# An earlier return of half of the lent adjacency, two loads moved behind other transfers and copies, and four more adjacency passes per node tile in the hyperedge stage

## The chip, the core and the metric

One Trainium2 chip, one core. The metric is device time in microseconds: the median of the runs of one kernel. One execution of each kernel was also taken with the hardware profiler, and all traces here are of such executions. The granted clock of TensorE is given as a share of full speed.

A core has five engines that run their own instruction streams in order: PE (TensorE, matmuls and transposes), DVE (VectorE), ACT (ScalarE), POOL (GpSimd) and SP (SyncE, which here only issues DMAs). ScalarE and GpSimd issue DMAs too. In the profile, SPq, ACTq and POOLq are the issuing instructions on those engines.

## The reference

Four graph layers follow one another on `x` (8 x 2048 nodes x 64 features), with one 2048 x 2048 adjacency matrix `adj` of zeros and ones. After each layer: `x = layernorm(x + layer(x))`.

```python
# layer 0: hypergraph attention (64 hyperedges, H is 2048 x 64), h = x @ W
alpha = softmax over the members of a hyperedge of leaky_relu(h @ a_node)
agg   = einsum('ben,bnf->bef', alpha, h)
beta  = sigmoid(h @ a_gn + agg @ a_ge)                     # per node and hyperedge
all_he = elu(beta * h + (1 - beta) * agg)
coefs1 = softmax over the hyperedges of a node of tanh(elu(agg) @ fcW + fcb) @ av
g     = einsum('bne,benf->bnf', coefs1, all_he)
industry = (adj / deg) @ (x @ W_ind)                       # an adjacency product
out   = softmax-weighted sum of the pair (industry, g)
# layer 1
out   = (dinv * (adj + I) * dinv) @ x @ W.T                # an adjacency product
# layer 2: supports I, adj, 2 adj^2 - I, softmax(relu(EE'))  (E: 2048 x 16)
weights = einsum('nd,dkio->nkio', E, weights_pool)         # a 256 x 64 matrix for each node
out   = einsum('bnki,nkio->bno', x_g, weights) + E @ bias_pool
# layer 3: three steps on v, whose row 0 is first set to a given value
v = relu(concat(v, adj @ v) @ W1.T + b1) @ W2.T + b2
```

## The kernel before

**Data.** The 8 x 64 columns of `x` are handled as four **pairs** `p` of two batches (128 columns), the 2048 nodes as four **chunks** `c` of 512, and a chunk as four tiles `t` of 128 nodes. `adj` stays on the chip, in float32r, as sixteen tiles of 128 x 2048: seven of their own (`LEND = 7`, lines 257 to 262) and eight (`LENT = 8`) in two large tiles `adj_more` with the tags `more0` and `more1`, allocated by `lent_tiles` (L260 to L266), and one more. In an adjacency product the left operand is split in a high and a low float32r part (`split`, L163 to L170: a copy on ScalarE, then a subtraction, the line of which is L168). A product of one pair is 2 chunks at a time, 16 tiles, 2 parts: 64 matmuls of 128 x 512 for half of it, 128 in all.

**What sets the order.** Nearly all instructions of TensorE, and those wrapped in `pin`, stay in the order in which the program writes them (`tc.keep_in_program_order`); a scheduler places the rest, among it most DMAs on SyncE. Two generators share TensorE with the rest of the work. `filler` yields single matmuls of adjacency products in the background; `fill(n)` (L421) takes n of them. Each one also calls `tick` (L318 on), which counts down deferred work: `after(n, f, ...)` runs f after n more matmuls, `later(n, f)` likewise but one after the other. Deferred work is placed by a count of matmuls, not by time, and a filler that has nothing ready yields "wait", in which case a tick passes and no matmul is issued.

**Hyperedge stage (60 to 226 us, L767 to L830).** For each node tile k of 16, and each slot s of it (a slot: the s-th hyperedge of each node), three matmuls make `pz`, then VectorE multiplies it by R (L818), ScalarE takes the exponential, VectorE finishes elu (L820) and weights it, GpSimd adds to `acc`. `fill(3)` (L807), once per tile, and `fill(5)` (L809), once per slot, put background matmuls between. Five slots before the end of a tile `slots(tiles[k + 2], ...)` (L814) prepares the tile after the next: a transpose `pslot` on TensorE, two copies on ScalarE (L288), then the one-hot matrices. `acc` is scattered to memory at the end of a tile.

**Mixing stage (226 to 476 us, L894 to L1104).** For each of 16 (pair, chunk) steps i the industry part is turned and scaled (`mix_ind`), g is loaded and turned (`mix_g`), both get scores (`mix_scores`, `mix_weigh`), and `mix_end` (L957 to L984) turns the mixture back: four transposes `pt`, then an addition on VectorE, the layernorm in steps (`normalized`), then a store of x1 by SyncE (L971). Between these, `fill(8)` or, past step 4, `fill(9)`, four times per step.

The background work in this stage is first the rest of the industry products of layer 0, then layer 1 (L1035): for each pair, two halves of 64 matmuls, tile by tile, from `part[p, c]`. That part is made by `l1_parts` (L986): a load of x1 (L992), a scale on GpSimd 16 matmuls later (L995), a cast in two pieces on ScalarE and VectorE 6 further on (L168). `while (p, t // JT) not in part: yield "wait"` (L1041) holds the generator until the cast of that chunk has been issued. At the end of a half two copies `ut` on ScalarE (L1058) empty the accumulators, and `l1_end` (L1009) follows by `later`: four matmuls `po`, an addition, a layernorm, a store of x2 by SyncE, and `load_xn` (L1028). Its three whole-pair loads of x2 (1 MB each, for the start of layer 2) are issued by ScalarE 14 matmuls later (L1033), once there is `room` for them (set behind the second step of a short loop, `make_el`, which fills 32 + 4 x 16 matmuls).

**Layer 2 (508 to 1263 us)** ends with a loop over 32 slots of per-node weights ("the chunk stage"): for each slot `form` builds weights in `w_half`, which lies in the space of `more0` and `more1` (`lend`, L1511; the adjacency tiles there have been stored to `adj_hbm`), and `multiply` uses them one slot later; `w_half` 0 belongs to even slots, 1 to odd ones. Per chunk, `pick` gathers the sums on VectorE, and `chunk_end` (L1577) stores them (`y_hbm`, L1584), loads them back transposed (L1596) with the residual `xb` (L1590), adds (L1602), squares (L1605), takes the power (L1609 to L1611), scales on VectorE in the last chunk (L1618 for x, L1621 for y) and stores x3 (L1623). `at(slot, period, f)` hangs such pieces on the quarters (periods) of a slot. `load_first` (L1634) loads tiles of x3's pair 0 back for layer 3; `first_turn` (L1630) turns one of its chunks.

What follows the loop (L1678 to L1689) is: the adjacency tiles are allocated again, eight DMAs on GpSimd return the first half of them, then the last chunk's `store` and `load` on SyncE, then eight DMAs on SyncE return the second half.

**Layer 3 (1263 to 1729 us).** `opening` (L1795 on) starts the first adjacency product with the tiles that were never lent; 28 matmuls in, the rest of the last `chunk_end` and `last_constants` are issued, the latter with two constants `more` on SyncE (L116), centred on VectorE (L128 to L132). The part of the product with tiles 7 to 11 uses the first returned half and one tile of the second; `first_turn(3)` (L1832) needs the last chunk of x3.

## Time and profile before

| | |
|---|---|
| median of 3 runs | 1728.79 us (1728.06 to 1730.58) |
| profiled execution, its own time | 1730.81 us |
| its span in the trace | 1729.0 us |
| mean granted clock | 0.989 |

The table of stages, from one view of the trace (busy time of an engine in a stretch, in us; the clock; the mean share in which the 16 DMA engines were busy):

| stretch, us | PE | DVE | ACT | POOL | clock | DMA |
|---|---|---|---|---|---|---|
| 0 to 60, degrees and scores of layer 0 | 40.93 | 43.80 | 13.17 | 22.26 | 0.94 | 0.82 |
| 60 to 226, hyperedges | 146.67 | 144.25 | 84.32 | 133.18 | 0.96 | 0.48 |
| 226 to 251.3, between | 23.56 | 7.66 | 9.99 | 8.50 | 1.00 | 0.48 |
| 251.3 to 476, mixing and layer 1 | 221.06 | 161.31 | 86.01 | 131.01 | 1.00 | 0.42 |
| 476 to 508, end of layer 1 | 26.81 | 14.66 | 7.23 | 8.28 | 0.89 | 0.45 |
| 508 to 1235, layer 2 | 723.30 | 291.59 | 285.63 | 203.82 | 1.00 | 0.39 |
| 1235 to 1282, its end, and layer 3's start | 39.36 | 15.30 | 6.08 | 14.02 | 0.96 | 0.77 |
| 1282 to 1729, layer 3 | 433.71 | 164.47 | 96.68 | 48.88 | 0.99 | 0.17 |

How to read what follows. In the list of waits a line such as "PE pz L172 <- DVE y L820: 5.5, 9, 1.2" says that TensorE, before instructions of line 172 that write `pz`, stood 5.5 us in all, in 9 places, at most 1.2 us in one, and that the last thing to come was VectorE's instruction of line 820. Line 172 is the helper for all matmuls and 175 the one for transposes, so the tile's name tells which they are; numbers are left out of tile names. A timeline line is: start, length, engine, line, operation, out<-in, then how often, and in brackets the idle time ahead of it with what ended it. A line of the view by stretches gives the stretch, its length, busy time (and count) of PE, PEld, DVE, ACT and POOL, the granted clock, the DMA share and GB/s.

### The profile page before, as it was taken

What the parts mean: (1) busy time and instruction counts of PE and PEld (TensorE: products, weight loads), DVE (VectorE), ACT (ScalarE), POOL (GpSimd) and SP (SyncE); (2) the same over time, 40 slices, a digit from 0 to 9 for tenths busy, and PEclk for the clock granted to TensorE, in tenths of its full rate; (3) what the DMA queues carried; (4) which work ended last, traced back from release to release, by engine and by line L of the source; (5) the groups of instructions that cost most, each with busy time, mean ns of one, the idle gap of its engine ahead of it and who ended that gap; (6) DMA issues with size and microseconds to landing.
All of it is one profiled execution on the core that took longest, in us unless ns stands there. A gap on an engine that the chain in (4) does not pass through costs nothing. (4 is left out here: it accounts for less than half of the span.)

```text
span 1729.0 us, 28043 instructions
## 1 busy us (share of the span) xinstructions
PE 1655.4 (96%) x11230; PEld 1208.0 (70%) x11230; DVE 843.0 (49%) x1536; ACT 589.1 (34%) x1033; POOL 569.9 (33%) x516
## 2 busy tenths in 40 slices
PE   6888899999989999999999999999989999999996
PEld 4666666666664444478888778888767877878775
DVE  7789945768742221210136157777533433433332
ACT  1355533344321212111213267878511221212221
POOL 3678845556534543422123001313210200202001
PEclk9899999999999999999999999999999999999998
DMA  9833334444330000027344457675571111211111
GB/s 341 277 134 125 121 131 138 146 147 146 117 118 1 31 31 1 24 71 296 113 134 140 118 137 158 138 168 126 171 242 48 50 55 43 62 48 42 57 43 39
DMA packets 171212, 195.83 MB, mean 113 GB/s; under 512 B 71568, under 2 KB 116368, under 8 KB 169792
## 3 DMA queue, kind: packets, MB, share of 16 engines
q1 hardware_dynamic: 160384, 154.61, 30.3%
q0 software_dynamic: 8544, 30.68, 5.3%
q10 hardware_dynamic: 2144, 8.65, 1.3%
q8 instruction: 90, 1.47, 0.4%
q14 instruction: 50, 0.41, 0.1%
HBM read 126.72 MB, written 67.17 MB: 112 GB/s over the span
## 5 line engine op out<-in xcount | busy, mean ns | idle before, releaser
L172 PE MATMUL ua<-pt,xn 128*128 128x512 f32 x512 | 230.2, 592 | 1.4 <-DVE pt L1177 1.4
L172 PEld LDWEIGHTS ua<-pt,xn 128*128 128x128 f32 x512 | 97.0, 190 | 111.0 <-issue 104.1
L1542 DVE COPY w_half<-pw 128x512 f32<-128x512 f32 x160 | 109.8, 705 | 87.8 <-PE pw L172 87.1
L1538 ACT COPY w_half<-pw 128x1024 f32<-128x1024 f32 x128 | 129.8, 1014 | 58.6 <-PE pw L172 58.5
L172 PE MATMUL py<-w_half,xg 128*32 128x128 f32 x4096 | 142.1, 279 | 3.1 <-issue 3.1
L172 PE MATMUL u<-adj,v0h 128*128 128x512 f32 (+1 forms) x388 | 135.7, 427 | 0.6 <-ACT h L1856 0.6
L172 PE MATMUL u<-adj,v0l 128*128 128x512 f32 (+1 forms) x388 | 125.8, 402 | 0.0
L172 PE MATMUL u<-adj_more,v2h 128*128 128x512 f32 (+1 forms) x388 | 125.7, 402 | 0.0
L172 PEld LDWEIGHTS py<-w_half,xg 128*32 128x32 f32 x4096 | 111.3, 138 | 20.5 <-issue 3.7
L172 PE MATMUL u<-adj_more,v2l 128*128 128x512 f32 (+1 forms) x388 | 124.0, 396 | 0.0
L1183 POOL TENSOR_TENSOR acc<-acc,pt 128x512 f32<-128x512 f32 x60 | 76.4, 1274 | 104.3 <-DVE pt L1177 103.7
L172 PE MATMUL pw<-est,wst 64*128 64x256 f32 x1024 | 109.8, 317 | 0.5 <-ACT w_half L1538 0.4
L1177 DVE TENSOR_SCALAR pt<-pt 128x512 f32<-128x512 f32 x64 | 29.8, 465 | 152.8 <-ACT pt L1176 152.7
L172 PEld LDWEIGHTS pw<-est,wst 64*128 64x128 f32 x1024 | 82.2, 185 | 25.4 <-ACT w_half L1538 18.7
L1757 ACT CAST ar<-fcav 128x512 fp32r<-128x512 f32 x64 | 39.6, 618 | 165.7 <-DMA fcav<-in_adj_t 164.8
L172 PE MATMUL u<-adj_more,v3l 128*128 128x512 f32 (+1 forms) x291 | 93.5, 396 | 2.1 <-DVE v3l L168 2.0
L1758 DVE SCALAR_TENSOR_TENSOR ar<-fcav,ar 128x512 f32<-128x512 f32 x64 | 45.6, 713 | 100.6 <-ACT ar L1757 100.6
L1176 ACT ACTIVATE pt<-s 128x512 f32<-128x512 f32 x64 | 38.0, 598 | 164.8 <-PE s L172 164.8
L172 PE MATMUL u<-adj,v1h 128*128 128x512 f32 (+1 forms) x291 | 94.0, 401 | 0.0
L172 PE MATMUL u<-adj_more,v3h 128*128 128x512 f32 (+1 forms) x291 | 93.1, 398 | 0.0
L172 PE MATMUL u<-adj,v1l 128*128 128x512 f32 (+1 forms) x291 | 92.6, 395 | 0.0
L1727 POOL TENSOR_TENSOR x<-x,rows 128x512 f32<-128x512 f32 x16 | 22.5, 1431 | 211.8 <-PE pt L175 200.5
(409 smaller groups left out, 3288.4 us busy)
## 6 DMA issues: line engine op xcount, KB each, us to landing
fcav<-in_adj_t SPq DMA_DIRECT2D x64, 256.0 KB, 2.9
u_hbm<-ut SPq DMA_DIRECT2D x48, 256.0 KB, 2.8
xg<-u_hbm SPq DMA_DIRECT2D x24, 512.0 KB, 7.0
adj<-in_adj_t POOLq DMA_DIRECT2D x16, 512.0 KB, 7.9
adj_more<-in_adj_t POOLq DMA_DIRECT2D x16, 512.0 KB, 7.9
adj_hbm<-adj_more SPq DMA_DIRECT2D x16, 512.0 KB, 6.1
x_hbm<-r SPq DMA_DIRECT2D x28, 256.0 KB, 2.3
hs_hbm<-st ACTq DMA_DIRECT2D x8, 584.0 KB, 5.9
```

Of the source, the lines that this page charges most:

```text
L172: tc.keep_in_program_order(nc.tensor.matmul(*args, **kw))
L1176: nc.scalar.activation(pt, s, AF.Exp)
L1177: nc.vector.tensor_scalar(pt, pt, 1.0, None, op0=ALU.max)
L1183: nc.gpsimd.tensor_tensor(accs[c], accs[c], pt, ALU.add)
L1538: pin(nc.scalar.copy(dst, pw.rearrange("p j o n -> p n (j o)")))
L1542: pin(copy(dst[:, :, 2 * j:2 * j + 2], bank.rearrange("p o n -> p n o")))
L1727: nc.gpsimd.tensor_tensor(xs, xs, b2.to_broadcast([P, JT, P]), ALU.add)
L1757: nc.scalar.copy(ar, seen_a)
L1758: nc.vector.scalar_tensor_tensor(ar.bitcast(F32), seen_a, 1.0, ar.bitcast(F32), op0=ALU.mult, op1=ALU.not_equal, accum_out=left[:, t, k:k ...
```

## The change

Three edits.

1. `lent_tiles` takes a number, so that each of the two large tiles can be allocated by itself. The first one is allocated, and its eight returning DMAs are issued, in the hook of the last slot (`SLOTS`, period 0), where the even-slot buffer `w_half` 0 has no further use but the product of the slot before; they now are on SyncE instead of GpSimd. The second stays where it was. `load_first(NT - 4, NT - 2)`, a load of two tiles of x3, moves from a hook of the last slot to behind the last chunk's `store` and `load`.
2. The three loads of x2 are no longer issued 14 matmuls after the last store of a pair, but collected, and issued behind the two copies `ut` of a half of layer 1; once the last half is through, at once.
3. In the hyperedge stage four more background matmuls follow each `slots(...)` in the loop.

```diff
-    def lent_tiles():
-
-        tiles = []
-        for i in range(2):
-            more = adj_pool.tile([P, LENT // 2, N], F32R, tag=f"more{i}", name="adj_more")
-            tiles += [column_halves(more[:, k, :]) for k in range(LENT // 2)]
-        return tiles
-
-    adj = [adj_tile(adj_pool, t) for t in range(LEND)] + lent_tiles()
+    def lent_tiles(i):
+
+        more = adj_pool.tile([P, LENT // 2, N], F32R, tag=f"more{i}", name="adj_more")
+        return [column_halves(more[:, k, :]) for k in range(LENT // 2)]
+
+    adj = [adj_tile(adj_pool, t) for t in range(LEND)] + lent_tiles(0) + lent_tiles(1)
...
                 if s == max(0, S - 5) and k + 2 < NT:
                     slots(tiles[k + 2], pps, "mm", 3)
+                    fill(4)
...
+    xn_loads, at_once = [], []
+
+    def begin_loads():
+        while xn_loads:
+            p = xn_loads.pop(0)
+            nc.scalar.dma_start(xn[p], x2_hbm[p][:])
+
     def load_xn():
 
         for p in range(NP - 1):
             if room and done[p] == NCH:
                 done[p] = 0
-                after(14, lambda p=p: nc.scalar.dma_start(xn[p], x2_hbm[p][:]))
+                xn_loads.append(p)
+        if at_once:
+            begin_loads()
...
                 pin(nc.scalar.copy(ut, u[c]))
                 later(6 + 8 * k, lambda p=p, c=c, ut=ut, x1=l1_load(p, c): l1_end(p, c, ut, x1))
+            if (p, g) == (NP - 1, 1):
+                at_once.append(True)
+            begin_loads()
...
-    at(SLOTS, 2, lambda: load_first(NT - 4, NT - 2))
...
+    def return_adj(tiles, eng):
+        for t in tiles:
+            for g in range(2):
+                pin(eng.dma_start(adj[t][g].bitcast(F32), adj_hbm[t - LEND, :, cols(g, N // 2)]))
+
+    def return_first():
+        adj[LEND:LEND + LENT // 2] = lent_tiles(0)
+        return_adj(range(LEND, LEND + LENT // 2), nc.sync)
+
+    at(SLOTS, 0, return_first)
...
     store, load, *waiting = ends[-1]
-    adj[LEND:LEND + LENT] = lent_tiles()
-
-    def return_adj(tiles, eng):
-        for t in tiles:
-            for g in range(2):
-                pin(eng.dma_start(adj[t][g].bitcast(F32), adj_hbm[t - LEND, :, cols(g, N // 2)]))
-
-    return_adj(range(LEND, LEND + LENT // 2), nc.gpsimd)
+    adj[LEND + LENT // 2:LEND + LENT] = lent_tiles(1)
     store()
     load()
+    load_first(NT - 4, NT - 2)
     return_adj(range(LEND + LENT // 2, LEND + LENT), nc.sync)
```

## The prediction

> **What bounds the kernel now.** I read the busy line of the page first, then the list of what TensorE waited for, then the timelines around the places that it names.

> ```profile
> PE 1655.4 (96%) x11230; PEld 1208.0 (70%) x11230; DVE 843.0 (49%) x1536; ACT 589.1 (34%) x1033; POOL 569.9 (33%) x516
> PE pz L172 <- DVE y L820: 5.5, 9, 1.2
> PE pz L172 <- DVE R L787: 3.0, 2, 2.2
> PE pz L172 <- ACT slot L288: 2.8, 4, 1.0
> PE po L172 <- ACT ut L1058: 5.5, 3, 3.7
> PE pt L175 <- DVE x L1618: 5.4, 2, 4.1
> PE u L172 <- DVE v3l L168: 2.0, 1, 2.0
> ```

> TensorE is the bound almost everywhere, so the change can only win or lose time where TensorE stands still. Three places matter: the hyperedge stage (60 to 226 us, waits of 18.9 us in all, the pz lines), the end of layer 1 (po, 3.7 us at once) and the end of the chunk stage (pt, then v3l). A second price goes with each stop. The granted clock in the stretches 484 to 492 us:

> ```profile
> 484.00:486.00 2.00, 0.00 (x0) 0.00 (x0) 0.31 (x1) 0.00 (x0) 0.00 (x0) 0.61 0.11 43
> 486.00:488.00 2.00, 0.75 (x3) 0.75 (x4) 0.00 (x0) 1.07 (x2) 0.00 (x0) 0.50 0.41 91
> 488.00:490.00 2.00, 2.00 (x10) 1.81 (x9) 0.64 (x1) 0.37 (x1) 0.00 (x0) 0.50 0.95 385
> ```

> The number ahead of the DMA share is the clock: 0.50 during and after the stop of 3.67 us that ends at 487.25. The same follows the stop of 3.06 us at 139.5 and the one of 4.1 us at 1268.3, but not the one of 2.16 us at 161.8 (clock 1.00). After the first, eight po matmuls and six passes took 4.25 us where they take 0.89 + 6 x 0.2335 = 2.3 elsewhere: 1.9 us lost. At 1270 the loss is 1.4 us. I take 1.7.

> A "pass" below is one 128x512 matmul of an adjacency product: two start 0.467 us apart, so 0.2335 us.

> **Part 1, the chunk stage's end.** SyncE's timeline, start and length of the issues:

> ```profile
> 1240.89 2.09 SPq L1623 DMA_DIRECT2D x_hbm<-y  x2
> 1249.94 0.34 SPq L1634 DMA_DIRECT2D x<-x_hbm  x1
> 1250.37 3.65 SPq L1584 DMA_DIRECT2D y_hbm<-sums  x4
> ...
> 1258.61 3.03 SPq L1596 DMA_DIRECT2D y<-y_hbm  x4
> ```

> The last picks end on VectorE at 1245.6, but the y stores wait in SyncE's queue behind load_first (L1634), which waits for the x3 store of the chunk before to land, until 1249.94. The landing is slow because GpSimd's eight returns of the adjacency (4.2 MB, issued 1241.8 to 1246.2) fill the DMA engines: share 1.02 to 1.03 from 1245 to 1260. The change moves load_first behind the y loads and the eight returns to SyncE, as soon as the buffer is free. The last product from w_half 0 starts at 1234.3, so they issue from 1235.4, 6.4 us sooner, at 0.55 us each (GpSimd's eight took 4.44, the other eight on SyncE 4.58): done at 1240, before the x3 store is ready (1240.9), in a stretch in which SyncE is idle. In the built order each y store also waits for one of the returns 3 to 6 to land; at some 410 GB/s number 6 lands near 1246, so that costs up to 1 us. y stores at 1246 instead of 1250.4; the y loads, landings and layernorm follow some 5.5 us sooner with fewer bytes in front. VectorE's last x (now ended at 1269.9) is then there at about 1264, when TensorE reaches its transposes (1263.8). The 5.4 us go, and the half clock's 1.4. What is late next is v3l (2.0 us): VectorE stands in order behind the weight `more`, whose DMA landed at 1279.0, 12.7 us after the last return was issued. Both it and TensorE's need move by 6 to 7 us. Bounds: nothing gained to all 2.0 gained; I take 1.6, since the second return drains with fewer bytes behind it. load_first itself lands by 1261 and is needed at 1263.8. **Part 1: -8.4 us**, from -3.5 (v3l grows) to -9.

> [...] The rows agree that the queue isn't the gain (4.44 against 4.58 us); the earlier start and the wait taken off SyncE are[...]. [...]

> **Part 2, the x loads at the end of layer 1.**

> ```profile
> 486.17 0.33 ACTq L1033 DMA_DIRECT2D xn<-x_hbm  x1
> 486.61 1.07 ACT L1058 COPY ut<-u 128x512 f32<-128x512 f32 x2 [7.96 <-issue]
> ```

> ScalarE waits at the third load for x2 to land, and its two copies wait behind it, then TensorE's po: 3.7 us, and 1.9 at half clock. In the built order the first copy now stands ahead of that load and the second behind it; po of the first is then free, and po of the second comes 8 passes later (1.9 + 0.9 us). The x2 stores are also issued ahead of two x1 loads that held SyncE for 4.35 us. Between 0 and -5.6; I take **-5.6**. The loaded tile is needed at the next stage, 20 us on, where the 1 MB load takes 6.3.

> **Part 3, fill(4).** It adds no work: fourteen times four of the 1088 passes are issued in the hyperedge stage instead of later, 56 x 0.2335 = 13.1 us. In that stage they cover waits, 16.7 us of which lie behind the first place. Tile by tile, four passes (0.93 us) meet waits of 2.7, 0.8, 1.2, 4.9, 0, 0, 2.2, 0, 0, 0.6, 0.3, 2.2, 0.9 and 0.8 us; what a tile cannot hide delays the next, and about 1.5 us are over at the end. VectorE (144 of 166 us busy) doesn't get more work, but a late pz starves it: 1 to 6 us. I take **+1.5**.

> Then the passes run out later. Layer 1 multiplies the output of the mixing, and a pass that needs a part (p, c) is issued only after the cast of that part. In the built order of before every fill of the mixing gets its 8 or 9 passes; in that of after 35 places stay empty, 6, 13 and 16 of them at the fourth part (t = 12) of pairs 0, 1, 2. There TensorE stands until the chain from the transposes pt of that chunk to its cast is through. Pair 3 of before shows this chain:

> ```profile
> 455.69 0.66 PE L175 MATMUL pt<-ident,ind 128*128 128x128 f32 x4 [1.17 <-DVE ind L960]
> 466.82 0.32 SPq L971 DMA_DIRECT2D x_hbm<-r  x1
> 469.62 0.32 SPq L992 DMA_DIRECT2D y<-x_hbm  x1
> 472.51 1.04 POOL L995 TENSOR_TENSOR y<-y,dinv 128x512 f32<-128x512 f32 x1 [0.51 <-DMA y<-x_hbm]
> 475.34 0.68 DVE L168 TENSOR_TENSOR v3l<-y,v3h 128x512 fp32r<-128x512 f32 x1
> ```

> pt to store took 6.9 to 12.7 us over the 16 chunks. Those without a cast ahead of the first addition on VectorE, as at pairs 1 and 2 in the built order of after, took 8.1 to 8.8: I take 8.5. Store to y load 2.8, load to GpSimd 2.9, scale 1.04, cast 0.65: **15.9 us**. TensorE's work between pt and the pass is now 34, 27, 24 and 42 passes, and beside them 5.06 us of mixing (a step is 13.47 us from pt to pt, less 36 passes), for pair 3 two po and the pt instead (2.3): 13.0, 11.4, 10.7 and 12.1 us. It stands for 2.9, 4.5, 5.2 and 3.8 us, 16.4 in all. Three are longer than the 3.06 that halved the clock: 3 x 1.7 = 5.1.

> [...] the trace has a halving at 3.06 and none at 2.16. [...] A fourth would add 1.7.

> Against this the later stages have 13.1 us fewer passes. **Part 3: 1.5 + 16.4 + 5.1 - 13.1 = +9.9 us.**

> **Sum.** -8.4 - 5.6 + 9.9 = -4.1 on the span of 1729.0. The profiled execution took 1730.8 in all, and the median of the runs is 1728.8, 0.2 under the span; so 1728.8 - 4.1 = 1724.7. A measurement of this kernel tells about 0.2% (3.5 us) from no change; the forecast lies just beyond.

> **Rivals.**
> A. *The mixing can't feed layer 1* (slower). At the fourth chunks themselves pt to store took 10.3, 11.1, 10.0 and 11.1 us, 10.6 in the mean. The chain is then 18.0, the stops 5.0, 6.6, 7.3 and 5.9 = 24.8, four at half clock 6.8: part 3 is +20.0, the sum +6.0, 1734.8. It decides from a chain of about 16.8 us, where the fourth halving comes in too. For it: the nearest rows by position. Against it: in before those chunks queue behind casts of the same pair, which stand elsewhere now. At pair 3's whole 19.7 us it is 1741.6.
> B. *One wait for another at the chunk stage's end* (no change). Part 1 gives -3.5 since the DMA of `more` or the staggered y stores hold VectorE and SyncE: sum +0.8, 1729.6. For it: DMA share 1.0 through that stretch. Against: the bytes start 6.4 us sooner.
> C. *The chain is short once TensorE isn't ahead of it* (much faster). With the shortest pt to store, 6.9, it is 14.3: stops 1.3, 2.9, 3.6, 2.2 = 10.0, one halving: part 3 is +0.1, sum -13.9, 1714.9.
> D. *The load isn't behind both copies.* It isn't, in the built order. If x2 lands late, part 2 gives -2 and the sum is -0.5, 1728.3.

> **How the numbers follow.** Forecast 0.38, A 0.34, C 0.12, B 0.09, D 0.07. Faster by over 0.2%: the forecast with a part cut off below, and C: 0.48. Slower: A, with a little of B: 0.36. The rest, 0.16. The range for 8 in 10 runs from C to the nearer part of A: 1715 to 1737; the forecast's own is 1720 to 1728.

> **What would show it.** Right: pz waits well under 10 us; no wait of pt for x at L1618, y stores right behind the picks; no ScalarE wait of 8 us ahead of ut; TensorE waits for v3h or v3l at four places of the mixing, 3 to 5 us each, with a clock of 0.5 behind them. Wrong: those waits are absent, or 6 us and longer (A); or the hyperedge stage grows by much more than 1.5 us.

## The result, and the profile after

| | before | changed |
|---|---|---|
| median, us | 1728.82 (1728.06 to 1730.58, 4 runs) | 1745.78 (1741.84 to 1748.34, 4 runs) |
| ratio, 95% interval | | 1.0099 (1.0084 to 1.0114) |
| profiled execution; its span | 1730.81; 1729.0 | 1745.67; 1743.9 |
| mean granted clock | 0.989 | 0.983 |

The changed kernel is slower by 17 us, where 4.1 us less were forecast, and it lies beyond the far end of the range. I cut both spans at the same instructions, which the traces give by name (us):

| from | to | before | changed | difference |
|---|---|---|---|---|
| start | first pz | 63.5 | 61.4 | -2.2 |
| first pz | first pi of the mixing | 162.5 | 167.5 | +4.9 |
| first pi | first pt | 25.3 | 26.8 | +1.5 |
| first pt | first ua (mixing, layer 1) | 256.7 | 273.2 | +16.5 |
| first ua | first u of layer 3 | 735.4 | 733.7 | -1.7 |
| first u of layer 3 | end | 485.6 | 481.4 | -4.2 |

The first and fifth rows hold no edit. Single executions of one kernel differ by several us (before: 1724.6 to 1735.4 in 47 runs), so differences of 2 us between two profiles say nothing alone. The fourth row does. By the profiles the whole difference is 14.9 us, by the medians 17.0.

The list of TensorE's waits in the changed kernel (total, times, longest) answers to the one shown of before:

```profile
PE u L172 <- ACT v3h L167: 16.6, 3, 6.3
PE u L172 <- ACT v2h L167: 8.8, 2, 6.0
...
PE pz L172 <- DVE y L818: 4.6, 6, 2.3
...
PE pt L175 <- DVE x L1628: 2.7, 2, 1.4
PE u L172 <- DVE v3l L168: 2.5, 2, 1.3
```

The first two lines are new: before had no wait of an adjacency product for v2h or v3h. TensorE stands 25.4 us for the casts of layer 1, as foreseen in kind but not in size, and not only at fourth chunks (v3) but twice at third ones (v2). The view by stretches, from the first pt to the first ua, gives for the kernel before:

```profile
251.35:508.04 256.69, 247.82 (x1118) 168.29 (x1117) 175.93 (x256) 93.29 (x165) 139.24 (x107) 0.99 0.42 139
```

and for the changed one:

```profile
255.62:528.80 273.18, 241.30 (x1062) 160.44 (x1061) 161.61 (x256) 93.35 (x162) 129.72 (x96) 0.94 0.39 129
```

TensorE does 56 matmuls fewer there (x1062), worth 13.1 us, but is busy only 6.5 us less. The other 6.6, a remainder, are put down to the clock (0.94 for 0.99). Its idle time went from 8.9 to 31.9 us. So +23.0 idle, +6.6 clock, -13.1 of passes: +16.5.

### The profile page after: what moved, and what is told of

Read it like the earlier page. It is cut to its first block, busy times and chain, and to the rows that moved or that the text cites. A ratio compares the mean times of both kernels' runs of the same rounds, so it can differ in the third digit from the quotient of the medians.

```text
span 1743.9 us, 28023 instructions
## 1 busy us (share of the span) xinstructions
PE 1659.3 (95%) x11230; PEld 1210.8 (69%) x11230; DVE 824.9 (47%) x1536; ACT 590.7 (34%) x1033; POOL 563.8 (32%) x508
## 5 line engine op out<-in xcount | busy, mean ns | idle before, releaser
L172 PE MATMUL ua<-pt,xn 128*128 128x512 f32 x512 | 230.2, 592 | 1.5 <-DVE pt L1187 1.5
L172 PEld LDWEIGHTS ua<-pt,xn 128*128 128x128 f32 x512 | 96.9, 190 | 111.1 <-issue 103.8
L172 PE MATMUL py<-w_half,xg 128*32 128x128 f32 x4096 | 141.4, 279 | 0.0
L172 PE MATMUL u<-adj,v0h 128*128 128x512 f32 (+1 forms) x388 | 134.6, 425 | 0.6 <-ACT h L1869 0.6
L172 PE MATMUL u<-adj_more,v2h 128*128 128x512 f32 (+1 forms) x388 | 126.1, 404 | 8.8 <-ACT v2h L167 8.8
L172 PE MATMUL u<-adj,v0l 128*128 128x512 f32 (+1 forms) x388 | 125.8, 401 | 0.0
L172 PE MATMUL u<-adj_more,v2l 128*128 128x512 f32 (+1 forms) x388 | 125.0, 398 | 0.0
L172 PEld LDWEIGHTS py<-w_half,xg 128*32 128x32 f32 x4096 | 111.0, 138 | 17.1 <-issue 0.2
L172 PE MATMUL pw<-est,wst 64*128 64x256 f32 x1024 | 110.5, 318 | 1.8 <-issue 1.0
L172 PE MATMUL u<-adj_more,v3h 128*128 128x512 f32 (+1 forms) x291 | 96.2, 408 | 16.6 <-ACT v3h L167 16.6
L172 PEld LDWEIGHTS pw<-est,wst 64*128 64x128 f32 x1024 | 82.5, 184 | 27.2 <-ACT w_half L1548 19.3
L172 PE MATMUL u<-adj_more,v3l 128*128 128x512 f32 (+1 forms) x291 | 94.6, 402 | 2.5 <-DVE v3l L168 2.5
L172 PE MATMUL u<-adj,v1h 128*128 128x512 f32 (+1 forms) x291 | 94.4, 401 | 0.0
L172 PE MATMUL u<-adj,v1l 128*128 128x512 f32 (+1 forms) x291 | 91.5, 393 | 0.0
```

The lines of the kernel that those rows point to most:

```text
L172: tc.keep_in_program_order(nc.tensor.matmul(*args, **kw))
```

## The experiments

All were timed beside the kernel before (1728.8 to 1729.2 in these batches).

| run | median, us | ratio to before (95%) |
|---|---|---|
| e1 parts 1 and 2, no added passes | 1724.5 | 0.9967 (0.9952 to 0.9981) |
| e2 added passes alone | 1751.8 | 1.0120 (1.0102 to 1.0138) |
| e3 part 1 alone | 1725.4 | 0.9984 (0.9974 to 0.9993) |
| e4 part 2 alone | 1727.7 | 0.9992 (0.9982 to 1.0002) |
| e5 changed, mixing fills 7/8 | 1721.2 | 0.9962 (0.9948 to 0.9976) |
| e6 changed, same count before the mixing | 1728.7 | 0.9997 (0.9987 to 1.0006) |
| e7 e1 with the early return on GpSimd | 1729.0 | 0.9997 (0.9988 to 1.0007) |
| e8 moved load of x3 alone | 1729.2 | 1.0002 (0.9993 to 1.0012) |
| e9 third x2 load on GpSimd | 1727.1 | 0.9986 (0.9974 to 0.9997) |
| e10 e1 with the returns last | 1732.0 | 1.0020 (1.0010 to 1.0029) |
| e11 changed, two added passes | 1733.1 | 1.0022 (1.0012 to 1.0032) |
| e12 changed, mixing fills 7 | 1722.7 | 0.9965 (0.9952 to 0.9977) |
| e13 e12 with the returns last | 1728.1 | 0.9995 (0.9982 to 1.0007) |
| e14 changed, later cast | 1743.5 | 1.0088 (1.0066 to 1.0111) |
| e15 e5, later cast | 1715.6 | 0.9920 (0.9908 to 0.9933) |

### Which part costs the time: e1 to e4

e1 leaves `fill(4)` out of the changed kernel; e2 puts it alone into the kernel before:

```diff
                     slots(tiles[k + 2], pps, "mm", 3)
+                    fill(4)
```

e3 is the kernel before with edit 1 of the change, e4 with edit 2.

> The changed kernel without the four added passes (parts 1 and 2 alone). Theory F (the passes issued sooner starve the mixing, and all of the loss is there): pt to ua takes about 4 us less than before's 256.7 us, the chunk stage's end (first u of layer 3 to the end of the span) 481.4 instead of 485.6, so about 1720.6 us, 8 under before. Theory L (the moved x loads or the new queue of the returns upset the order of deferred work in the mixing, and the fill is innocent): the stops for v3h and v2h stay, 1735 us or more. By the prediction's terms (8.4 and 5.6) it would be 1714.8.

> The kernel before with the four added passes alone. Theory F: hyperedge stage about 5 us longer, mixing with five stops of 3 to 6 us for v3h and v2h, each with the clock at 0.5 behind it, pt to ua about 20 us longer: about 1753 us. Theory L: mixing without such stops, hyperedge stage 5 us longer and later stages up to 13 us shorter: 1721 to 1735. By the prediction's own term for this part (+9.9): 1738.7.

> The kernel before with the earlier return on SyncE and the moved load of x3 alone (part 1). If the trace of after shows it rightly (y stores issued at the end of the picks, but 7.6 us for four of them): first u of layer 3 to the end 481.4 us instead of 485.6, about 1724.6. By the prediction: 1720.4. If after's gain there was chance: 1728.8.

> The kernel before with the moved x2 loads alone (part 2). By the prediction the stop of 3.7 us and its half clock go: 1723.2. If the second copy, still behind a load, takes its place with about 2 us (in after po waited for ut for 1.7 us at that point, at full clock): about 1725. If nothing is gained: 1728.8.

The added passes cost 22.9 us alone (e2) and 21.3 beside the rest (e1 against the changed kernel); parts 1 and 2 gain 3.5 and 1.2 by medians, 4.5 together. Theory F holds, L falls: e2's trace has the same five stops in the mixing (16.8 us for v3h, 8.7 for v2h, longest 6.4 and 6.0), and e1's has none. The gain of e1, 4.5 us, is smaller than the 8 us that its text expected.

e4 also shows that the edit of part 2 doesn't do what it says there. ScalarE's timeline in e4:

```profile
484.78 0.33 ACTq L1033 DMA_DIRECT2D xn<-x_hbm  x1
485.22 1.07 ACT L1067 COPY ut<-u 128x512 f32<-128x512 f32 x2 [6.58 <-DMA x_hbm<-r]
```

The loads aren't pinned, and in the order that was built the third one again stands ahead of both copies. The copies wait 6.58 us there instead of 7.96, and po 2.35 instead of 3.67. A half clock follows all the same, but a shorter one (3.4 us for 6.8):

```profile
488.00:490.00 2.00, 2.00 (x6) 1.52 (x6) 0.20 (x1) 0.63 (x1) 1.11 (x1) 0.50 0.66 262
```

### What the added passes do: e5, e6, e11, e12

The way of a part, in the changed kernel, from three timelines at step 3 (the fourth chunk of pair 0). TensorE's first, from the turned mixture pt to the pass that waits:

```profile
293.22 0.60 PE L175 MATMUL pt<-ident,ind 128*128 128x128 f32 x4
...
311.19 1.22 PE L172 MATMUL u<-adj_more,v3h 128*128 128x512 f32 x2 [4.38 <-ACT v3h L167]
```

SyncE between them (the store of x1, the load of y):

```profile
302.79 0.32 SPq L969 DMA_DIRECT2D x_hbm<-r  x1
...
305.33 0.42 SPq L990 DMA_DIRECT2D y<-x_hbm  x1
```

and VectorE, between pt and that store:

```profile
293.86 0.69 DVE L978 SCALAR_TENSOR_TENSOR r<-pt,r 128x512 f32<-128x512 f32 x1
...
295.31 0.69 DVE L875 SCALAR_TENSOR_TENSOR ln_c<-ln_m,r 128x512 f32<-128x512 f32 x1
298.81 0.69 DVE L168 TENSOR_TENSOR v2l<-y,v2h 128x512 fp32r<-128x512 f32 x1 [2.82 <-ACT v2h L167]
299.42 0.68 DVE L881 TENSOR_REDUCE ln_v<-r 128x8 f32<-128x512 f32 x1
```

From 293.22 to 311.19 are 18.0 us, 9.6 of them up to the store. The layernorm of this chunk stands still on VectorE for 2.8 us, behind the cast of the chunk before, which is ahead of it in program order and has no data yet. At step 7 the same cast of the third chunk stands right behind the first addition and waits 1.07 us. There pt begins at 355.67, the store is issued at 366.37 and the pass begins at 373.65, behind a stop of 5.93:

```profile
358.71 1.09 DVE L168 TENSOR_TENSOR v2l<-y,v2h 128x512 fp32r<-128x512 f32 x1 [1.07 <-ACT v2h L167]
366.37 0.32 SPq L969 DMA_DIRECT2D x_hbm<-r  x1
```

Read off in the same way, the ways that end in the five stops took 18.0 (step 3, stop 4.4), 18.0 (step 7, 5.9), 24.3 (step 10, 2.7), 20.5 (step 11, 6.3) and 22.3 us (step 14, 6.0). At step 14 it is GpSimd: the scale stands behind the layernorm of the next step. Its timeline there:

```profile
490.36 2.10 POOL L883 TENSOR_TENSOR ln_r<-ln_e,neg_half 128x8 f32<-128x8 f32 x1
492.43 1.04 POOL L993 TENSOR_TENSOR y<-y,dinv 128x512 f32<-128x512 f32 x1
```

e5 and e12 take fewer passes in the mixing, e6 takes fewer in the hyperedge stage, e11 adds two instead of four:

```diff
 e5:  -        k = 9 if i > NCH else 8
      +        k = 8 if i > NCH else 7
 e12: +        k = 7
 e6:  -                fill(5)          (once per slot)
      +                fill(4)
 e11: -                    fill(4)      (behind slots)
      +                    fill(2)
```

> The changed kernel with 7 and 8 passes per filling of the mixing instead of 8 and 9. Theory F (the passes run out because the feeding chain of 18 us is longer than what TensorE has to do until then): at the fourth part of each pair TensorE is now some 30 passes less far, no stop over 3 us for v2h or v3h; beside the version without the four passes (1724.5) hyperedges +4.5, later stages -13.1: 1716, or up to 1722 where short stops stay. Theory H (the four passes cost time where they stand, through VectorE in the hyperedge stage and what it defers): no change from after, about 1746.

> The changed kernel with 7 passes per filling throughout the mixing. With 7 and 8 one stop of 4.8 us for v3h stayed, at the last pair, and a half clock behind it. Theory F: some 40 passes (9.3 us) more are left for the last pair, the stop and its half clock go: 1721.2 - 4.8 - 1.7 = 1715. Rival (at 11.6 us a step the mixing's own chain on VectorE and ScalarE becomes the bound): new waits for ind, t or th of several us: 1721 or more.

> The changed kernel with four background passes per slot instead of five in the hyperedge stage, so that with the four added ones this stage issues 1 pass fewer than before, in other places. Theory F (it is the number of passes taken ahead of the mixing that counts): no stops in the mixing, hyperedge stage within 3 us of before's 162.6, about 1724.5 as without the added passes. Theory P (it is the place: behind the turning of slots the passes hold up pz): hyperedge stage 167 us, 1729 or more; if the stops in the mixing came with the place too, 1745.

> The changed kernel with two added passes per tile instead of four. Theory F (a stock of passes that runs out: a threshold): 28 passes or 6.5 us more lie ahead of each fourth part than in the changed kernel, so its stops of 4.4, 5.9, 6.3 and 6.0 us nearly go; hyperedges +2.5, later stages -6.5: 1720 to 1722. Theory H (each added pass costs in its place): half of the 21.3 us that the four cost: 1735.

With passes held back in the mixing the whole loss is gone: 1721.2 and 1722.7. That is 3 and 2 us under e1, but the intervals overlap e1's, so a gain of the added passes over leaving them out is not shown. The stretch from pt to ua is 246.7 us in e5 and 245.6 in e12 (e1: 255.3). e5 kept one stop for v3h, of 4.8 us, at the last pair. e12 lost it, but isn't faster than e5: its profile shows 5.6 us of waits for `ind` (e5: 1.6) and a stop of 3.0 at po, so the rival in its text came true in part. That profile is of an execution 9 us faster than e12's median, so it may not show what the usual one loses.

e6 falls between F and P. No pass of it waits for v2h or v3h, so the count decides these stops; but it is 4 us slower than e1. In the traces 2.9 of that are the place: its hyperedge stage takes 165.6 us (e1: 162.7). The mixing is 4.4 us longer too, half of it at the copies at the end of layer 1, where po stands 4.5 us (2.3 in e1); other stretches are shorter. Over the traces, the hyperedge stage of the seven other kernels with four passes there took 164.4 to 167.5 us, 166.1 in the mean, that of the eight with none 161.1 to 163.2, 162.4 in the mean: the four passes cost 3.7 us there. With two (e11) it was 166.3.

e11 missed: 1733.1, near to H's number, but not for H's reason. By H, half of the passes cost half, but the stage was as long as with four. Its stops for v2h and v3h are two, the first longer than any in the changed kernel:

```profile
PE u L172 <- ACT v3h L167: 7.5, 1, 7.5
PE u L172 <- ACT v2h L167: 6.0, 1, 6.0
```

They lie at steps 11 and 14; pairs 0 and 1 have none. I had subtracted 6.5 us from each stop of the changed kernel, as if all were paid from one stock. But a stop gives passes back: in the changed kernel each one let the mixing catch up, so that the later pairs began with no more behind them than in e11. With fillings of 9 the stock falls by 4 passes a step (32 are fed), in every kernel; how many were added sets the pair at which it is gone, and from then on each pair pays in full. This reading comes from the positions of the stops and the counts of passes; no run tests it by itself.

### The chunk stage's end: e3, e8, e7, e10

SyncE's timeline in the changed kernel:

```profile
1254.62 6.12 SPq L1674 DMA_DIRECT2D adj_more<-adj_hbm  x8
1260.83 2.90 SPq L1633 DMA_DIRECT2D x_hbm<-y  x2
1265.02 7.58 SPq L1594 DMA_DIRECT2D y_hbm<-sums  x4
...
1274.99 2.54 SPq L1606 DMA_DIRECT2D y<-y_hbm  x4
```

The y stores begin right behind the picks (which end at 1264.7), as foreseen, but the four issues take 7.58 us, where before took 3.65. The y loads come 2.7 us sooner (15.2 us behind the first u of layer 3 in before, 1258.61 - 1243.44, and 12.5 here, 1274.99 - 1262.53), not 5.5.

```diff
 e8:  load_first behind load(), the returns as before (GpSimd, ahead of store())
 e7:  return_adj(range(LEND, LEND + LENT // 2), nc.gpsimd)   # in return_first
 e10: -    at(SLOTS, 0, return_first)
      +    return_first()                                    # behind load_first
```

> The kernel before with the load of x3 moved behind the last y loads, and the returns as before on GpSimd, issued 1241.8 to 1246 us. If the moved load is what brings part 1's 3.5 us: 1725.4. If it needs the earlier return (the y stores, sent off at 1246 with eight returns just issued, take 7 us as they do behind the early return, and the y loads come no sooner than in before): 1728 to 1729.

> Parts 1 and 2 with the eight early returns on GpSimd instead of SyncE. Theory Q (on SyncE each y store waits for a return eight issues ahead of it to land, so four stores take 7.6 us): stores issued within 4 us of the picks, y loads some 4 us sooner than on SyncE, no wait of pt for x, first u of layer 3 to the end 479 us instead of 483.5: about 1720.5. Theory B (the DMA engines are full until 1270 us, so nothing lands sooner whoever issues it): as on SyncE, 1724.5.

> Parts 1 and 2 (no added passes), with the early return of the first half put behind the last chunk's stores and loads. Theory B2 (while returns are under way, the issue of a y store itself takes up to 3 us; with the DMA engines idle it takes 0.5): four y stores in about 2 us instead of 7, y loads 5 us sooner, no wait of pt for x and no half clock behind it; the wait for v3l (3.0) stays, as the constant more is issued behind sixteen returns: 1720.5 against 1724.5. Rival (the bytes are needed early): TensorE waits for adjacency tiles 7 to 11 for 5 us or more: 1726 or more.

> All together: four added passes, 7 passes per filling, returns behind the last stores and loads. If the gains of the two parts (about -6 from 1721.2 and -4) add up: 1711. If only one of them comes: 1715 to 1718.

In e8 GpSimd issues the returns (first line) and SyncE the y stores behind them:

```profile
1240.72 4.44 POOL L1683 DMA_DIRECT2D adj_more<-adj_hbm  x8
```

```profile
1244.61 6.72 SPq L1584 DMA_DIRECT2D y_hbm<-sums  x4
```

In e10 no return is under way at that time:

```profile
1243.16 2.19 SPq L1593 DMA_DIRECT2D y_hbm<-sums  x4
...
1247.84 2.54 SPq L1605 DMA_DIRECT2D y<-y_hbm  x4
...
1251.09 15.20 SPq L1673 DMA_DIRECT2D adj_more<-adj_hbm  x16
```

So theory Q fell: in e7 the y stores have no return of SyncE's ahead of them, and their four issues still took 6.92 us, one of them 3.1. The slow issues go with the returns under way: four y stores cost 2.2 us of issue in e10, where the DMA engines' share was 0.02 from 1242 to 1244, and 6.7 to 7.6 behind 4.2 MB of returns, whoever issued those. What holds the issue is not shown: in before the four took 3.65 at a share of 1.02, behind a load that had waited for the x3 stores of the same queue to land. B2 is right in the price, and e10's pt waits for nothing. But the returns are then late: TensorE waits 3.3 us for adjacency tiles and 4.8 for v3l (the constant `more` is issued at 1269.9, behind sixteen returns), with half clocks behind, and e10 is 7.5 us slower than e1, e13 5.4 slower than e12 (e13's text expected 1711 to 1718). e8 gains nothing. The moved load needs the early return, and the early return slows the stores that the moved load sets free. That e7 is 4.6 us slower than e1 stays open: its profiled execution (1722.7) was its fastest and shows no place for it.

### The copies at the end of layer 1: e9

```diff
-                after(14, lambda p=p: nc.scalar.dma_start(xn[p], x2_hbm[p][:]))
+                eng = nc.gpsimd if p == NP - 2 else nc.scalar
+                after(14, lambda p=p, eng=eng: eng.dma_start(xn[p], x2_hbm[p][:]))
```

> The kernel before with one edit: the last of the three x2 loads is issued by GpSimd instead of ScalarE, so that the two copies ut have no load ahead of them. If the stop of 3.7 us and its half clock are worth what the prediction took: no wait of po for ut at 484 us and 5.6 us less, 1723.3. If the copies wait for something else next (they share their buffer with a bias that is stored): 1.5 to 2.5 us less, about 1727. If GpSimd's wait holds up what is behind it: 1729 or more.

With no load ahead of them the copies wait for something else. ScalarE in e9:

```profile
482.88 0.59 ACT L1059 COPY ut<-u 128x512 f32<-128x512 f32 x1 [6.59 <-DMA bias_hbm<-bias]
```

`ut` and `bias` share two buffers, so the copy waits for the store of a bias; po stands 2.33 us, without a half clock behind it, and 1.8 us are gained:

```profile
484.00:486.00 2.00, 2.00 (x14) 1.73 (x13) 0.69 (x1) 0.86 (x2) 1.17 (x2) 1.00 0.26 29
```

### The cast's place: e14, e15

```diff
-        after(16, scale, 6 if (p, c) != (NP - 1, 0) else 16, cast)
+        after(16, scale, 14 if (p, c) != (NP - 1, 0) else 16, cast)
```

> The changed kernel with one number changed: the cast of a part of layer 1 is issued 14 matmuls behind its scale instead of 6, so that on VectorE it stands behind the variance of the next chunk's layernorm instead of ahead of it. Theory C (the layernorm of the fourth chunk waits in order behind the cast of the third, 2.8 us in one place): the way from pt to the store of the fourth chunks falls from 9.6 to 12.9 us to 8 to 10, each of the four stops is about 2.5 us shorter, one or two half clocks go: 1745.8 - 10 - 2 = about 1734. Theory D (the chain is long because its engines are busy, and order plays no part): no change within 2 us, 1744 to 1748.

> The version with 7 and 8 passes per filling (1721.2) with the same later cast. It has one stop of 4.8 us left at the last pair. Theory C: this stop falls to about 2.3 us and its half clock goes: 1717. Theory D: 1721.

In e14 step 3 goes from pt to store in 7.5 us instead of 9.6, and the three stops for v3h fell from 4.4, 5.9 and 6.3 to 2.5, 4.3 and 3.6 us, as theory C has it. But step 7 took 14.2 to its store, third chunks now stop for 2.4, 3.0 and 4.6 us, and the last pair for 2.2 and 2.7 on top: 25.3 us of stops in all, for 26.7, and the time, 1743.5, is not clearly another than the changed kernel's. The cast's order is a part of the length of the way, then, but not what sets the sum. Where the stock lasts (e15) the median is 5.6 us under e5's: 1715.6, the fastest version here, 0.8% under before. Theory C named that gain in size, but not rightly in kind. The last stop fell from 4.8 to 3.6 us only, and its half clock stayed:

```profile
PE u L172 <- ACT v3h L167: 3.6, 1, 3.6
470.00:472.00 2.00, 1.85 (x4) 1.34 (x5) 0.95 (x3) 0.61 (x2) 0.58 (x1) 0.50 0.39 131
```

The stretch from pt to ua is 2.1 us shorter than e5's. Where the rest comes from is not shown, since other stretches, which hold no edit, are shorter as well.

## Why the prediction was wrong

- **"What bounds the kernel", right where the traces reach.** What they could place lies where TensorE stands, runs at half clock or takes passes at another time; no other stage moved beyond what single executions differ by. The 4.6 us of e7 and a part of e15's gain could not be placed.
- **Part 3, +9.9, came out at +22.9 (e2); the -13.1 of passes and the places of the stops were right in kind.** Stops at the fourth parts of pairs 0, 1 and 2 were named, with half clocks behind them (that of pair 3, 3.8 in the prediction, came as 1.3). **The step that failed is the chain of 15.9 us**, in it "pt to store: I take 8.5", and with it the choice of the forecast over rival A. Measured were 9.6 and 10.7 us to the store at the first two stops and 18.0 in all, to a tenth what A assumed (at the first, 1.0 of the 2.1 us lay behind the store: the load and the cast took 8.4 for 7.4). A's threshold was 16.8. The prediction looked for a cast ahead of VectorE's *first addition* and found none. The cast stood behind it: at step 3 between the layernorm's subtraction and its variance, where it waited 2.8 us, at step 7 right behind the addition, where it waited 1.1. With the cast moved (e14) step 3 fell to 7.5, but step 7 rose to 14.2, so this order explains the first stop's way and not the second's.
- **A is no full account either; two things were left out.** Third chunks: steps 10 and 14 stopped too (2.7 and 6.0 us), which no term had. That a chain held back by one stop is late for the next is a reading, not shown; step 14's scale queued on GpSimd. Stops, 16.4 in the prediction, were 25.4 for v2h and v3h and 1.3 for a v3l. The clock, net of the halving at 484 us that went, was +3.2 in the sum (5.1 - 1.9) and measured +6.6, with four stops at half clock for two stretches of 3.4 us each and one for one.
- **"I take +1.5" for the hyperedge stage: too small.** Measured +3.7 over all traces. The added passes hid 6.2 us of waits (idle 18.5 to 12.3 between first pz and first pi), not the 11.6 assumed (busy time rose by 11.1, for 13.1 of passes); and e6 shows that four passes at this place cost 2.9 us even when the stage has none more in all.
- **Part 1, -8.4: right way, too large.** It gave -3.5 by the medians (e3; -1.2 to -4.5 by the interval), the near end of its range. SyncE's idle stretch did hide the eight issues, and the stores left with the picks. The failed term is "that costs up to 1 us" for the staggered y stores: their issues took 7.6 us, for 3.65 in before. Rival B named them, with -3.5. The prediction compared the two queues by the returns' own issue only (4.44 us on GpSimd, 4.58 on SyncE). The stores behind the returns are slow with either: with the returns on GpSimd their four issues took 6.92 us (e7) and 6.72 (e8).
- **Part 2, -5.6: failed.** It gave -1.2 (e4; its interval includes none). I had read the built order of the whole change, in which the third load falls between the copies; without the added passes it falls ahead of both. And I named no next wait for the copies: the bias store, seen in e9.
- **The sum.** Against -4.1, the terms were off by +10.3 (idle time from pt to ua, the stop at 484 us within it), +3.4 (clock there), +3.4 (hyperedges), +1.5 (up to the first pt) and +4.2 (part 1); the stretches without an edit came out 3.8 shorter, no more than single executions differ by. That is 19.0 in all, which makes of -4.1 the +14.9 of the two spans.

## What to carry to other kernels

Background work that fills waits early is taken from a stock: before adding it, find the place where the stock runs out and compare the latency of what feeds it, measured at that place, with the work left ahead of it. If it is short, hold back as many fillers downstream as were added upstream; here this turned +17 us into -8 (e5), and with a later cast into -13 (e15), where the kernel without the added passes had -4.5 (e1). Read a latency chain off the built order of *every* instruction between its ends, not only the first, since one in-order wait in the middle can lengthen the whole chain (at step 3 VectorE waited 2.8 us; with the cast moved, pt to store took 7.5 us for 9.6).

## What the runs showed of the hardware

```profile
408.57:411.99 3.42, 1.45 (x10) 0.97 (x8) 2.51 (x5) 2.08 (x4) 0.67 (x1) 1.00 0.69 228
411.99:415.40 3.41, 3.41 (x11) 1.48 (x10) 1.29 (x2) 0.55 (x1) 2.00 (x2) 0.50 0.45 156
425.64:429.05 3.41, 1.56 (x8) 0.99 (x8) 1.58 (x2) 0.62 (x1) 2.37 (x3) 1.00 0.00 0
429.05:432.47 3.42, 3.42 (x17) 1.92 (x15) 3.32 (x8) 1.15 (x3) 1.71 (x1) 1.00 0.59 192
```

- Over all 17 traces (65 to 1700 us), steps at full clock in which TensorE was busy for less than 40% were followed by half clock in 58 of 58 cases, those with 75% or more in 0 of 7725, those between in 26 of 212 (in before and the changed kernel alone: 9 of 9, 0 of 903, 3 of 25). So in these traces the price of a stop went with how much of one step it left idle. An estimate from these counts and the measured 3.413 us: with TensorE busy around it, a stop of 4.1 us or more leaves some step busy for less than 40% wherever it falls, and pays; one under 0.85 us leaves every step busy for 75% or more, and does not; between them it is a chance times a loss, not a limit in us as the prediction had it.
